# Cross-attention and FFN layer: keys of the first two batches on POOL's queue, one root in the token norm, VectorE in source order, full last key chunks

## The chip, the cores and the metric

The kernel runs on one core of a Trainium2 chip. The metric is device time in microseconds (us) of one execution, as the median of three runs. The profile is one further execution on the same chip. Engines: PE (TensorE), DVE (VectorE), ACT (ScalarE), POOL (GpSimd) and SP (SyncE, which here only issues DMAs); PEld is PE's weight load.

## What is computed

Input x is 8 batches of 100 tokens of width 512 (800 tokens); the context is 8 batches of 722 rows of width 512, with a mask of padded rows. The layers, cut to what matters:

```python
x = x + align(ctx, layernorm(x))       # dynamic programming over 722 by 100 rows, rows of ctx summed along the path
x = x + moe(layernorm(x))              # 16 experts (relu, hidden width 1024), the best 3 of each token by their gates
ln = layernorm(layernorm(x)) * g + b   # a norm of a norm, then gain and bias
xn = layernorm(ctx) * gx + bx
q = rms(ln @ W_q)                      # 8 heads of 64; q and k are normed per head
k, v = rms([xn; ln] @ W_k), [xn; ln] @ W_v
p = softmax(where(mask, q @ k.T, -max))  # 722 context keys, masked, and the batch's own 100 tokens: 822 keys
x = x + (p @ v) @ W_out + b_out        # cross-attention
x = x + ffn(layernorm(x))              # relu, width 2048, 4 experts that differ by a term of rank 4, the best 2
```

All is float32.

## The kernel before

The span falls into stages that follow one another on PE: alignment, with the keys and values of the context computed beside it (to about 600 us); the 16 experts (to 945); the token stage of the cross-attention (979 to 1098); the attention loop (to 1300); the FFN (to the end). A scheduler sets the order of instructions on each engine from the source and its own estimates, except where the source opens a `manual_schedule` for an engine: there that engine follows the source. The attention loop has one for PE, DVE and ACT. Each engine works off its own instructions in order, and waits in order.

**From the experts to the tokens.** Experts' rows go through DRAM: each row block is written to `ys_d` on POOL's queue (L835), and the token stage gathers, for every token, its three rows. Rows over an expert's capacity would be worked off under `tc.If(some > 0)` (L856); in these runs nothing is over, so the branch is passed by, but all engines wait at it. What stands ahead of the If on ACT or SP must be done before any engine goes on.

**`load(b)`** (L907 to L916) begins a batch of the attention: it clears the padding columns of the keys' tile `akt` (L909, POOL), loads 722 keys from `k_d` (L910, SP, 1444 KB), loads the mask words `mw` (L912, SP, the same words to 100 partitions), clears the mask tile `mb` beyond column 722 (L914, POOL) and turns the mask into 0 or minus the largest float (L915, ACT). `akt` has three buffers, `mw` and `mb` two. `early = [load(b) for b in range(2)]` stands ahead of the token loop in the source. The scheduler put these two, and the keys' load of the third batch, ahead of the If.

**The token loop** (L973 to L1066) takes seven tiles of up to 128 tokens. For tile t: three gathers `back` (L978, indirect DMAs on POOL's queue, four buffers), each added into X with its gate on DVE (L982); BN statistics and the norm of the norm, with two roots on ACT (L992, L995) and small DVE steps between them (L993 to L998); `xn` (L1000, DVE); four transposes `pt` (L1003, PE); `xT` (L1005, ACT, four); queries and keys `pqk` (L1013, PE, eight products); squares `asq` (L1015, ACT), their sums `rq` (L1017, DVE), a root (L1018, ACT), a maximum and a reciprocal (DVE), `qn` (L1022, DVE); transposes `apt` (L1030, PE); `qt` and `kl` (L1034, L1036, ACT), `kl` written to `k_d` (L1041, SP). Values `apv` of each batch whose tokens are complete (L1049, PE, one PSUM buffer), `avr` (L1054, DVE), written to `v_d` (L1055, SP). From t = 2 on, two heads' scores `psc` of the first batch (L933, PE) and their row maxima `junk` (L943, DVE). After the loop: `negated` (PE, ACT), `pbo` (L1068, PE), `bo` (L1071, DVE), the seven additions of `bo` into X (L1074, POOL). Then come loads of FFN weights `at_`, `wi` (L1078, L1082, SP), `mt` (L1089, SP) and `mk` from it (L1091, DVE).

**The attention loop** has 32 steps (8 batches by 4 pairs of heads). A step makes the scores `pst` in two groups of key chunks (4 and 3 chunks of 128 keys), adds the negated maxima (`et`, L1123, DVE), takes Exp per chunk (L1129, ACT), sums over chunks (`two`, `ws`, L1153 to L1160, POOL) and multiplies the step before by the values (`apo`, L1141, PE). The chunks start at

```python
STARTS = (0, 128, 256, 384, 512, 640, S2)
```

with S2 = 722, so chunk 5 has 82 keys and chunk 6 the 100 own tokens; `values` loads these two in four pieces (L1103). After two steps `pws` (L1167, PE) spreads the sums.

Of the kernel before, what the change touches and what calls it, by code (L numbers as in the profile page):

```python
# [9 lines left out]
F32 = mybir.dt.float32  # L10
U8 = mybir.dt.uint8
I32 = mybir.dt.int32
AF = mybir.ActivationFunctionType
ALU = mybir.AluOpType
# [3 lines left out]
P = 128  # L18
B, S, D = 8, 100, 512
# [13 lines left out]
KEYS = S2 + S  # L33
MW = (S2 + 3) // 4
KG = ((0, 4), (4, 7))
# [9 lines left out]
KP, KC = 128, 7  # L45
KW = S2 + KP
STARTS = (0, 128, 256, 384, 512, 640, S2)
NCH, CW = 15, 49
# [8 lines left out]
def rows_of(c):  # L57
    return P if c < RC - 1 else RLAST


def key_rows(c):
    return (*STARTS, KEYS)[c + 1] - STARTS[c]


def tok_rows(t):
    return P if t < NT - 1 else NTOK - (NT - 1) * P
# [3 lines left out]
def kernel(  # L70
# [46 lines left out]
    qgs = const.tile([P, 1], F32, name="qgs")  # L117
    nc.vector.tensor_scalar_mul(qgs, gcol[:, 0:1], DH ** -0.5)

    X = state.tile([P, NT, D], F32, name="X")  # L120
# [773 lines left out]
    if True:  # L894
# [8 lines left out]
        if True:  # L903
            ak = attn.enter_context(tc.tile_pool(name="attnk", bufs=2, side="right"))

            def load(b):

                kt = ak.tile([P, NPAIR, KW], F32, tag="akt", name="akt", bufs=3)
                nc.gpsimd.memset(kt[:, :, KEYS:], 0.0)  # L909
                nc.sync.dma_start(out=kt[:, :, :S2], in_=k_d[b, :, :, :S2])  # L910
                mw = ak.tile([S, MW], I32, tag="mw", name="mw")
                nc.sync.dma_start(out=mw, in_=mask[b].partition_broadcast(S))  # L912
                mb = ak.tile([S, KEYS], F32, tag="mb", name="mb")
                nc.gpsimd.memset(mb[:, S2:], 0.0)  # L914
                nc.scalar.activation(mb[:, :S2], mw.bitcast(U8)[:, :S2], AF.Copy, bias=-FMAX, scale=FMAX)  # L915
                return dict(b=b, kt=kt, mb=mb)  # L916
# [5 lines left out]
            def tokens(st):  # L922

                nc.sync.dma_start(out=st["kt"][:, :, S2:KEYS], in_=k_d[st["b"], :, :, S2:])

# [39 lines left out]

            early = [load(b) for b in range(2)]
            with tc.tile_pool(name="qkv", bufs=2, side="right") as qp:
                nc.sync.dma_start(out=wo, in_=w_out.rearrange("(c p) n -> p c n", p=P))
                nc.sync.dma_start(out=bo, in_=b_out.partition_broadcast(P))
                eps = qp.tile([P, 1], F32, name="eps", bufs=1)  # L970
                nc.gpsimd.memset(eps, EPS)
                given = 0
                for t in range(NT):  # L973
                    n = tok_rows(t)
                    cols = ds(t * P, n)
                    for k in range(TOPK):
                        back = qp.tile([P, D], F32, tag="back", name="back", bufs=4)
                        nc.gpsimd.indirect_dma_start(  # L978
                            out=back[:n], out_offset=None, in_=ys_d,
                            in_offset=bass.IndirectOffsetOnAxis(ap=seen[:n, t, k : k + 1], axis=0), bounds_check=NROW,  # L980
                        )
                        nc.vector.scalar_tensor_tensor(  # L982
                            X[:n, t, :], back[:n], gk[:n, t, k : k + 1], X[:n, t, :], ALU.mult, ALU.add
                        )
# [4 lines left out]
                    nc.vector.bn_aggr(mv, st)  # L989
                    rr = qp.tile([P, 4], F32, tag="rr", name="rr")  # L990
                    one, var, two, shift = (rr[:, i : i + 1] for i in range(4))
                    nc.scalar.activation(one, mv[:, 1:2], AF.Sqrt, bias=eps)  # L992
                    nc.vector.reciprocal(one, one)  # L993
                    nc.vector.scalar_tensor_tensor(var, mv[:, 1:2], one, one, ALU.mult, ALU.mult)
                    nc.scalar.activation(two, var, AF.Sqrt, bias=eps)  # L995
                    nc.vector.reciprocal(two, two)
                    nc.vector.tensor_tensor(two, two, one, ALU.mult)
                    nc.vector.scalar_tensor_tensor(shift, mv[:, 0:1], -1.0, two, ALU.mult, ALU.mult)  # L998
                    xn = qp.tile([P, D], F32, tag="xn", name="xn")
                    nc.vector.tensor_scalar(xn, X[:, t, :], two, shift, ALU.mult, ALU.add)  # L1000
                    pt = aps.tile([P, D], F32, tag="tr", name="pt", bufs=1)
                    for dc in range(DC):
# [54 lines left out]
                    if t < 2:  # L1057
                        tokens(early[t])
                    else:
                        st, hp = early[(t - 2) // NPAIR], (t - 2) % NPAIR  # L1060
                        for i, ps in enumerate(scores(st, hp)):
                            largest(st, hp, i, ps)
                for part in range(3):
                    negated(early[0], part)
# [31 lines left out]
            def values(st):  # L1096
                b = st["b"]
                va = at.tile([KP, KC, D], F32, tag="va", name="va")
                nc.sync.dma_start(
                    out=va[:, : KC - 2, :], in_=v_d[b, : STARTS[KC - 2], :].rearrange("(c p) d -> p c d", p=KP)  # L1100
                )
                for c, r0, r1 in ((KC - 2, 0, 80), (KC - 2, 80, key_rows(KC - 2)), (KC - 1, 0, 96), (KC - 1, 96, S)):
                    nc.sync.dma_start(out=va[r0:r1, c, :], in_=v_d[b, STARTS[c] + r0 : STARTS[c] + r1, :])  # L1103
                st["va"] = va
# [14 lines left out]
            def weights(st, hp, c0, c1, ps):  # L1119
# [7 lines left out]
                for c in range(c0, c1):  # L1127
                    n = key_rows(c)
                    nc.scalar.activation(et[:n, c - c0], et[:n, c - c0], AF.Exp, bias=mk[:n, b, c : c + 1])  # L1129
                return et  # L1130

            def products(st, hp, c0, c1, et):
# [4 lines left out]
                for c in range(c0, c1):  # L1137
                    n = key_rows(c)
                    for i in range(2):
                        h = 2 * hp + i  # L1140
                        nc.tensor.matmul(  # L1141
                            st["po"][i * DH : (i + 1) * DH, hp, :], st["va"][:n, c, h * DH : (h + 1) * DH],
                            et[:n, c - c0, i, :], start=c == 0, stop=c == KC - 1,
                        )

            def sums(st, hp, c0, c1, et):
# [8 lines left out]
                two = st["two"]  # L1155
                nc.gpsimd.tensor_tensor(two[:, 0], two[:, 0], et[:, 0], ALU.add)
                nc.gpsimd.tensor_tensor(ws[:, hp], two[:, 0], two[:, 1], ALU.add)
                for c in (1, 2):
                    n = key_rows(KG[1][0] + c)
                    nc.gpsimd.tensor_tensor(ws[:n, hp], ws[:n, hp], et[:n, c], ALU.add)  # L1160

# [274 lines left out]
def _layout(i):  # L1436
# [5 lines left out]
    mask[:, :S2] = np.ascontiguousarray(f["mask_BxS2_bk0"]).view(np.uint8)  # L1442
    keys = np.ones((B, KC + 1, KP), np.uint8)
    keys[:, : KC - 1].reshape(B, -1)[:, :S2] = mask[:, :S2]
    a_t = np.zeros((D, P), np.float32)
# [50 lines left out]
```

## Time and profile before

| | |
|---|---|
| median of 3 runs | 1538.27 us (1536.83 to 1538.72) |
| profiled execution | 1538.33 us |
| its span | 1536.6 us |
| mean granted TensorE clock | 0.949 |
| busy share of the span | PE 90%, DVE 45%, ACT 32%, POOL 28% |
| mean DMA rate | 142 GB/s |

Times of the profile count from the start of the span. A busy PE need not be PE at full clock: the clock that was granted has its own column.

### The profile page before, as it was taken

How to read it: one execution, taken by the hardware profiler on the slowest of the kernel's cores; microseconds unless marked ns; L12 is line 12 of the kernel's file. 1: busy time of each engine (PE TensorE's matmuls, PEld its weight loads, DVE VectorE, ACT ScalarE, POOL GpSimd, SP SyncE). 2: the span in 40 equal slices, each digit the busy share in tenths (PEclk: the TensorE clock that was granted, in tenths of full speed). 3: DMA queues.
4: the chain of work that ended last, by engine and by line, in shares of the span. 5: the costliest groups of instructions: out<-in, count | busy, mean ns of one | idle time of the engine just before them, and what ended most of it. 6: DMA issues, size and time to landing. Idle time of an engine off the chain costs nothing. (4 is left out here: it accounts for less than half of the span.)

```text
span 1536.6 us, 19541 instructions
## 1 busy us (share of the span) xinstructions
PE 1385.6 (90%) x7043; PEld 870.6 (57%) x7043; DVE 684.9 (45%) x1492; ACT 485.2 (32%) x1506; POOL 436.1 (28%) x552
## 2 busy tenths in 40 slices
PE   5979887989799998999999996499999997899998
PEld 4443333444333543899999995144476765544433
DVE  3579999799723251101100100634477773322220
ACT  3424354554522554121122221132354543200000
POOL 1014333545423356000000000600365554322210
PEclk8989899999999998899999998699899999999999
DMA  9861213542655143866567786521544420400000
GB/s 307 298 169 38 78 51 109 167 122 71 207 169 158 56 163 139 291 245 237 204 228 250 260 291 237 143 48 35 194 139 133 134 89 1 164 0 0 1 23 21
DMA packets 120857, 217.78 MB, mean 142 GB/s; under 512 B 47765, under 2 KB 49077, under 8 KB 120629
## 3 DMA queue, kind: packets, MB, share of 16 engines
q1 hardware_dynamic: 103413, 152.54, 30.9%
q0 software_dynamic: 16464, 61.44, 11.5%
q10 hardware_dynamic: 880, 2.51, 0.5%
q8 instruction: 58, 0.95, 0.3%
q14 instruction: 42, 0.34, 0.1%
HBM read 163.92 MB, written 50.86 MB: 140 GB/s over the span
## 5 line engine op out<-in xcount | busy, mean ns | idle before, releaser
L720 PE MATMUL pk<-wc,ctk 128*128 128x512 f32 x384 | 191.9, 641 | 25.8 <-ACT vr L726 22.7
L720 PE MATMUL pv<-wc,ctk 128*128 128x512 f32 x384 | 176.1, 597 | 0.0
L807 PE MATMUL ph<-xe,w1t 128*128 128x192 f32 (+4 forms) x1024 | 171.5, 314 | 1.3 <-DVE xe L798 1.3
L822 PE MATMUL py<-hT,w2t 128*128 128x192 f32 (+4 forms) x1024 | 169.7, 310 | 0.0
L807 PEld LDWEIGHTS ph<-xe,w1t 128*128 128x128 f32 x1024 | 154.4, 192 | 4.7 <-DVE xe L798 1.7
L822 PEld LDWEIGHTS py<-hT,w2t 128*128 128x128 f32 x1024 | 153.1, 191 | 1.8
L720 PEld LDWEIGHTS pk<-wc,ctk 128*128 128x128 f32 x384 | 76.9, 205 | 123.6 <-issue 92.8
L737 ACT ACTIVATE kjunk<-k 128x64 f32<-128x64 f32 x384 | 98.0, 255 | 111.3 <-POOL k L725 95.5
L811 ACT ACTIVATE hT<-ph,b1t 128x192 f32<-128x192 f32 (+4 forms) x128 | 51.8, 404 | 253.4 <-PE ph L807 253.4
L720 PEld LDWEIGHTS pv<-wc,ctk 128*128 128x128 f32 x384 | 73.1, 191 | 91.6 <-issue 88.6
L1129 ACT ACTIVATE et<-et,mk 128x200 f32<-128x200 f32 (+2 forms) x224 | 85.8, 451 | 67.2 <-DVE et L1123 67.1
L725 POOL TENSOR_TENSOR k<-k,kbias 128x512 f32<-128x512 f32 x48 | 71.9, 1503 | 99.1 <-ACT k L724 98.9
L798 DVE COPY xe<-px 128x768 f32<-128x768 f32 (+4 forms) x16 | 14.0, 875 | 185.8 <-PE ph L807 170.4
L835 POOL DMA_DIRECT2D ys_d<-yr x28 | 15.3, 547 | 285.8 <-ACT yr L834 285.8
L1356 PE MATMUL fpb<-xT,wi 128*128 128x400 f32 x256 | 91.5, 507 | 1.0 <-DVE z L1378 1.0
L1405 PE MATMUL fpo<-wot,hw 128*128 128x512 f32 x192 | 84.8, 595 | 0.0
L750 POOL TENSOR_TENSOR k<-k,rk 128x512 f32<-128x512 f32 x48 | 63.7, 1353 | 60.2 <-DVE rk L747 60.2
L440 DVE SCALAR_TENSOR_TENSOR junk<-two_i,path,C 8x735 f32<-8x735 f32 x64 | 74.1, 1157 | 9.7 <-DMA C<-step_d 7.7
L1113 PE MATMUL pst<-qt,akt 64*128 64x100 f32 x896 | 66.3, 282 | 6.8 <-DVE et L1123 6.7
L737 ACT ACTIVATION_READ_ACCUMULATOR kjunk<-k 128x1 f32 x384 | 72.0, 188 | 0.0
L1356 PEld LDWEIGHTS fpb<-xT,wi 128*128 128x128 f32 x256 | 47.0, 190 | 42.5 <-issue 9.4
L943 DVE CUSTOM_DVE_ANT_0 junk<-psc,mb 100x822 f32<-100x822 f32 x64 | 64.2, 1003 | 13.6 <-PE psc L933 13.3
(334 smaller groups left out, 2031.3 us busy)
## 6 DMA issues: line engine op xcount, KB each, us to landing
w1t<-in_w SPq DMA_DIRECT2D x16, 2048.0 KB
w2t<-in_w SPq DMA_DIRECT2D x16, 2048.0 KB
ct<-in_context_t SPq DMA_DIRECT2D x8, 1444.0 KB
ctk<-in_context_t POOLq DMA_DIRECT2D x8, 1444.0 KB
akt<-k_d SPq DMA_DIRECT2D x8, 1444.0 KB
cr<-in_context SPq DMA_DIRECT2D x8, 1280.0 KB
va<-v_d SPq DMA_DIRECT2D x8, 1280.0 KB
v_d<-vr POOLq DMA_DIRECT2D x8, 768.0 KB
```

The costliest lines, as they stand in the source:

```text
L440: nc.vector.scalar_tensor_tensor(junk, two_i1, path[:, j + 1 : j + 2], scol, ALU.is_le, ALU.mult, accum_out=path[:, j : j + 1])
L720: nc.tensor.matmul(ps, ct[:, dc, c * P : (c + 1) * P], wc[:, dc, lo : lo + D], start=dc == 0, stop=dc == DC - 1)
L725: nc.gpsimd.tensor_tensor(kc, kc, kbias, ALU.add)
L737: nc.scalar.activation(junk, k[:, c, h * DH : (h + 1) * DH], AF.Square, accum_out=rk[:, c, h : h + 1])
L750: nc.gpsimd.tensor_tensor(kh, kh, rk[:, c, :].unsqueeze(2).to_broadcast([P, NH, DH]), ALU.mult)
L807: nc.tensor.matmul(ph[:, :cap], st["w1t"][:, dc, hc * P : (hc + 1) * P], st["xe"][:, dc, :cap], start=dc == 0, stop=dc == DC - 1,)
L822: nc.tensor.matmul(py[:, dc, :cap], st["w2t"][:, hc, (2 * dh + dc) * P : (2 * dh + dc + 1) * P], st["hT"][:, hc, :cap], start=hc == 0, sto ...
L943: nc.vector.tensor_tensor_reduce(out=junk, in0=ps.rearrange("p b c -> p (b c)")[:S, :KEYS], in1=st["mb"], scale=1.0, scalar=-FMAX, op0=ALU ...
L1113: nc.tensor.matmul(ps[:, i, (c - c0) * S : (c - c0 + 1) * S], st["kt"][rows, hp, STARTS[c] : STARTS[c] + KP], qt[rows, hp, b * S : (b + 1) ...
L1129: nc.scalar.activation(et[:n, c - c0], et[:n, c - c0], AF.Exp, bias=mk[:n, b, c : c + 1])
L1356: nc.tensor.matmul(pb[:, :N2], wi[fc * P // FQ][:, dc, fc * P % FQ : fc * P % FQ + P], xT[:, dc, hh * N2 : (hh + 1) * N2], start=dc == 0, ...
L1405: nc.tensor.matmul(po[:n], hw[:, fc, t * P : t * P + n], wot[:, fc, :], start=fc == 0, stop=fc == FC - 1)
```

## The change

- `load` takes a queue. The first two batches are now loaded inside the token loop: the keys go out on POOL's queue (`nc.gpsimd`), each issued after the last gather of the next tile (`tc.issue_after`); the mask words stay on SP.
- The keys' tile is 822 wide, without padding columns; the mask word array holds the 100 own tokens too, and so `mb` is written by one activation of 822 columns. The memsets of both are gone.
- The norm of the norm takes one root: variance v gives 1/sqrt((1 + e) v + e e), with e = 1e-5, in place of a root, a reciprocal, a product and a second root and reciprocal. The memset of `eps` moves to the kernel's start.
- In the token loop DVE follows the source. The source takes the gathers, additions and norm of tile t + 1 (`gathered`) ahead of tile t's other work.
- The last two chunks are full: they start at 594 and 694 and overlap their neighbours; the key mask hides the repeated keys. Values load in three pieces instead of five, Exp and products take 128 rows throughout, and the sums of the second group take three POOL operations instead of four.

In the changed program SP's and POOL's orders follow from this: ahead of the If SP issues only the four mask loads; the third batch's keys are SP's first issue after it. POOL issues gathers 1 to 6, keys of batch 0, gathers 7 to 9, keys of batch 1, gathers 10 to 21. PE's, ACT's and DVE's orders in the token stage change too: on PE, `pt` of tile t + 1 and `apt` of tile t follow `pqk` of tile t after one `psc`, and `apv` comes later; on ACT, `xT` of t + 1 stands ahead of the root of `rq` of t; on DVE, `mk` stands ahead of `bo`.

```diff
--- before.py
+++ after.py
@@ -31,7 +31,7 @@
 NH, DH = 8, 64
 NPAIR = NH // 2
 KEYS = S2 + S
-MW = (S2 + 3) // 4
+MW = (S2 + S + 3) // 4
 KG = ((0, 4), (4, 7))
 FE, FF, FTOPK, FR = 4, 2048, 2, 4
 FC = FF // P
@@ -43,8 +43,8 @@
 RC = 6
 RLAST = S2 - (RC - 1) * P
 KP, KC = 128, 7
-KW = S2 + KP
-STARTS = (0, 128, 256, 384, 512, 640, S2)
+
+STARTS = (0, 128, 256, 384, 512, S2 - KP, KEYS - KP)
 NCH, CW = 15, 49
 LANES = NCH + 1
 LAG = NCH - 1
@@ -56,10 +56,6 @@
 
 def rows_of(c):
     return P if c < RC - 1 else RLAST
-
-
-def key_rows(c):
-    return (*STARTS, KEYS)[c + 1] - STARTS[c]
 
 
 def tok_rows(t):
@@ -116,6 +112,9 @@
     nc.sync.dma_start(out=gcol, in_=gamma_cols)
     qgs = const.tile([P, 1], F32, name="qgs")
     nc.vector.tensor_scalar_mul(qgs, gcol[:, 0:1], DH ** -0.5)
+
+    eps = const.tile([P, 1], F32, name="eps")
+    nc.gpsimd.memset(eps, EPS * EPS)
 
     X = state.tile([P, NT, D], F32, name="X")
     nc.gpsimd.memset(X[:, NT - 1, :], 0.0)
@@ -903,16 +902,14 @@
         if True:
             ak = attn.enter_context(tc.tile_pool(name="attnk", bufs=2, side="right"))
 
-            def load(b):
-
-                kt = ak.tile([P, NPAIR, KW], F32, tag="akt", name="akt", bufs=3)
-                nc.gpsimd.memset(kt[:, :, KEYS:], 0.0)
-                nc.sync.dma_start(out=kt[:, :, :S2], in_=k_d[b, :, :, :S2])
+            def load(b, queue=nc.sync):
+
+                kt = ak.tile([P, NPAIR, KEYS], F32, tag="akt", name="akt", bufs=3)
+                queue.dma_start(out=kt[:, :, :S2], in_=k_d[b, :, :, :S2])
                 mw = ak.tile([S, MW], I32, tag="mw", name="mw")
                 nc.sync.dma_start(out=mw, in_=mask[b].partition_broadcast(S))
                 mb = ak.tile([S, KEYS], F32, tag="mb", name="mb")
-                nc.gpsimd.memset(mb[:, S2:], 0.0)
-                nc.scalar.activation(mb[:, :S2], mw.bitcast(U8)[:, :S2], AF.Copy, bias=-FMAX, scale=FMAX)
+                nc.scalar.activation(mb, mw.bitcast(U8)[:, :KEYS], AF.Copy, bias=-FMAX, scale=FMAX)
                 return dict(b=b, kt=kt, mb=mb)
 
 
@@ -921,7 +918,7 @@
             nc.vector.tensor_copy(sel[DH:], ident[DH:, DH : DH + NH].unsqueeze(2).to_broadcast([DH, NH, KP]))
             def tokens(st):
 
-                nc.sync.dma_start(out=st["kt"][:, :, S2:KEYS], in_=k_d[st["b"], :, :, S2:])
+                nc.sync.dma_start(out=st["kt"][:, :, S2:], in_=k_d[st["b"], :, :, S2:])
 
             def scores(st, hp):
 
@@ -963,19 +960,17 @@
                     )
                 nc.scalar.copy(st["nb"][:, :, i, :], pm[:, : NPAIR * S].rearrange("p (c n) -> p c n", c=NPAIR))
 
-            early = [load(b) for b in range(2)]
+            early = []
             with tc.tile_pool(name="qkv", bufs=2, side="right") as qp:
                 nc.sync.dma_start(out=wo, in_=w_out.rearrange("(c p) n -> p c n", p=P))
                 nc.sync.dma_start(out=bo, in_=b_out.partition_broadcast(P))
-                eps = qp.tile([P, 1], F32, name="eps", bufs=1)
-                nc.gpsimd.memset(eps, EPS)
                 given = 0
-                for t in range(NT):
+                def gathered(t):
+
                     n = tok_rows(t)
-                    cols = ds(t * P, n)
                     for k in range(TOPK):
                         back = qp.tile([P, D], F32, tag="back", name="back", bufs=4)
-                        nc.gpsimd.indirect_dma_start(
+                        got = nc.gpsimd.indirect_dma_start(
                             out=back[:n], out_offset=None, in_=ys_d,
                             in_offset=bass.IndirectOffsetOnAxis(ap=seen[:n, t, k : k + 1], axis=0), bounds_check=NROW,
                         )
@@ -987,17 +982,27 @@
                     mv = qp.tile([P, 2], F32, tag="mv", name="mv")
                     nc.vector.bn_stats(st, X[:, t, :])
                     nc.vector.bn_aggr(mv, st)
-                    rr = qp.tile([P, 4], F32, tag="rr", name="rr")
-                    one, var, two, shift = (rr[:, i : i + 1] for i in range(4))
-                    nc.scalar.activation(one, mv[:, 1:2], AF.Sqrt, bias=eps)
-                    nc.vector.reciprocal(one, one)
-                    nc.vector.scalar_tensor_tensor(var, mv[:, 1:2], one, one, ALU.mult, ALU.mult)
-                    nc.scalar.activation(two, var, AF.Sqrt, bias=eps)
+                    rr = qp.tile([P, 2], F32, tag="rr", name="rr")
+                    two, shift = rr[:, 0:1], rr[:, 1:2]
+                    nc.scalar.activation(two, mv[:, 1:2], AF.Sqrt, scale=1.0 + EPS, bias=eps)
                     nc.vector.reciprocal(two, two)
-                    nc.vector.tensor_tensor(two, two, one, ALU.mult)
                     nc.vector.scalar_tensor_tensor(shift, mv[:, 0:1], -1.0, two, ALU.mult, ALU.mult)
                     xn = qp.tile([P, D], F32, tag="xn", name="xn")
                     nc.vector.tensor_scalar(xn, X[:, t, :], two, shift, ALU.mult, ALU.add)
+                    return xn, got
+
+                hand = tc.manual_schedule(engines={mybir.EngineType.DVE})
+                hand.__enter__()
+                xns = {0: gathered(0)}
+                for t in range(NT):
+                    n = tok_rows(t)
+                    cols = ds(t * P, n)
+                    if t + 1 < NT:
+                        xns[t + 1] = gathered(t + 1)
+                    if t < 2:
+                        with tc.issue_after(xns[t + 1][1].ins):
+                            early.append(load(t, nc.gpsimd))
+                    xn = xns.pop(t)[0]
                     pt = aps.tile([P, D], F32, tag="tr", name="pt", bufs=1)
                     for dc in range(DC):
                         nc.tensor.transpose(pt[:, dc * P : (dc + 1) * P], xn[:, dc * P : (dc + 1) * P], ident)
@@ -1060,6 +1065,7 @@
                         st, hp = early[(t - 2) // NPAIR], (t - 2) % NPAIR
                         for i, ps in enumerate(scores(st, hp)):
                             largest(st, hp, i, ps)
+                hand.__exit__(None, None, None)
                 for part in range(3):
                     negated(early[0], part)
 
@@ -1097,10 +1103,10 @@
                 b = st["b"]
                 va = at.tile([KP, KC, D], F32, tag="va", name="va")
                 nc.sync.dma_start(
-                    out=va[:, : KC - 2, :], in_=v_d[b, : STARTS[KC - 2], :].rearrange("(c p) d -> p c d", p=KP)
-                )
-                for c, r0, r1 in ((KC - 2, 0, 80), (KC - 2, 80, key_rows(KC - 2)), (KC - 1, 0, 96), (KC - 1, 96, S)):
-                    nc.sync.dma_start(out=va[r0:r1, c, :], in_=v_d[b, STARTS[c] + r0 : STARTS[c] + r1, :])
+                    out=va[:, : KC - 2, :], in_=v_d[b, : (KC - 2) * KP, :].rearrange("(c p) d -> p c d", p=KP)
+                )
+                for c in (KC - 2, KC - 1):
+                    nc.sync.dma_start(out=va[:, c, :], in_=v_d[b, STARTS[c] : STARTS[c] + KP, :])
                 st["va"] = va
 
             def raw_scores(st, hp, c0, c1):
@@ -1125,8 +1131,7 @@
                     st["nb"][:, hp].unsqueeze(2).to_broadcast([KP, 2, nk, S]), ALU.add,
                 )
                 for c in range(c0, c1):
-                    n = key_rows(c)
-                    nc.scalar.activation(et[:n, c - c0], et[:n, c - c0], AF.Exp, bias=mk[:n, b, c : c + 1])
+                    nc.scalar.activation(et[:, c - c0], et[:, c - c0], AF.Exp, bias=mk[:, b, c : c + 1])
                 return et
 
             def products(st, hp, c0, c1, et):
@@ -1135,12 +1140,11 @@
                     po = aps.tile([P, D], F32, tag="po", name="apo", bufs=1)
                     st["po"] = po[:, : NPAIR * S].rearrange("p (c n) -> p c n", c=NPAIR)
                 for c in range(c0, c1):
-                    n = key_rows(c)
                     for i in range(2):
                         h = 2 * hp + i
                         nc.tensor.matmul(
-                            st["po"][i * DH : (i + 1) * DH, hp, :], st["va"][:n, c, h * DH : (h + 1) * DH],
-                            et[:n, c - c0, i, :], start=c == 0, stop=c == KC - 1,
+                            st["po"][i * DH : (i + 1) * DH, hp, :], st["va"][:, c, h * DH : (h + 1) * DH],
+                            et[:, c - c0, i, :], start=c == 0, stop=c == KC - 1,
                         )
 
             def sums(st, hp, c0, c1, et):
@@ -1153,11 +1157,9 @@
                     nc.gpsimd.tensor_tensor(st["two"], et[:, 0:2], et[:, 2:4], ALU.add)
                     return
                 two = st["two"]
-                nc.gpsimd.tensor_tensor(two[:, 0], two[:, 0], et[:, 0], ALU.add)
+                nc.gpsimd.tensor_tensor(two, two, et[:, 0:2], ALU.add)
                 nc.gpsimd.tensor_tensor(ws[:, hp], two[:, 0], two[:, 1], ALU.add)
-                for c in (1, 2):
-                    n = key_rows(KG[1][0] + c)
-                    nc.gpsimd.tensor_tensor(ws[:n, hp], ws[:n, hp], et[:n, c], ALU.add)
+                nc.gpsimd.tensor_tensor(ws[:, hp], ws[:, hp], et[:, 2], ALU.add)
 
             def spread(st, j):
 
@@ -1440,8 +1442,12 @@
     cols = lambda v: v.reshape(-1, P).T
     mask = np.zeros((B, 4 * MW), np.uint8)
     mask[:, :S2] = np.ascontiguousarray(f["mask_BxS2_bk0"]).view(np.uint8)
-    keys = np.ones((B, KC + 1, KP), np.uint8)
-    keys[:, : KC - 1].reshape(B, -1)[:, :S2] = mask[:, :S2]
+    mask[:, S2:KEYS] = 1
+    keys = np.zeros((B, KC + 1, KP), np.uint8)
+    for c, s in enumerate(STARTS):
+
+        new = max(STARTS[c - 1] + KP if 0 < c < KC - 1 else S2 if c else 0, s) - s
+        keys[:, c, new:] = mask[:, s + new : s + KP]
     a_t = np.zeros((D, P), np.float32)
     b_t = np.zeros((P, FF), np.float32)
     for e in range(FE):
```

## The prediction

> **What bounds the kernel now.** I read the page's slices first. PE is 90% busy over the span, so only stretches in which PE idles can be won. The row of the granted clock falls to 6 in one slice alone (961 to 999 us): the way from the experts' last product into the cross-attention. So I asked for the waits of 940 to 980 us (engine, line, releaser: total, times, longest):
>
> ```profile
> PE pt L1003 <- DVE xn L1000: 33.5, 1, 33.5
> ...
> POOL eps L971 <- DMA akt<-k_d: 13.7, 1, 13.7
> ...
> ACT mb L915 <- DMA mw<-in_mask: 11.7, 2, 8.1
> ```
>
> PE stands still for 33.5 us, POOL for 13.7 of them. The timeline tells the chain (start, duration, engine):
>
> ```profile
> 946.01 0.54 SPq L910 DMA_DIRECT2D akt<-k_d  x1
> 946.55 0.54 POOL L835 DMA_DIRECT2D ys_d<-yr  x1 [1.15 <-ACT yr L834]
> 946.59 1.04 SPq L912 DMA_DIRECT2D mw<-in_mask  x1
> ...
> 958.80 0.81 ACT L915 ACTIVATE mb<-mw 100x722 f32<-100x722 uint8 x1 [3.63 <-DMA mw<-in_mask]
> 960.74 0.10 POOL L971 MEMSET eps<- 128x1 f32 x1 [13.65 <-DMA akt<-k_d]
> 961.56 1.14 POOL L978 DMA_INDIRECT back<-ys_d,seen  x1 [0.72 <-issue]
> ...
> 969.07 0.69 DVE L988 BATCH_NORM_STATS2 st<-X 128x6 f32<-128x512 f32 x1
> ...
> 979.08 1.09 PE L1003 MATMUL pt<-ident,xn 128*128 128x128 f32 x4 [33.49 <-DVE xn L1000]
> ```
>
> The small mask loads mw share the DMA engines with two 1444 KB loads of keys and land 8.7 and 12.2 us after issue. mb2 ends at 959.61, ACT and SP pass the If, all engines go on at 960.2, the first gather is issued at 961.56. The first tile's norm takes 9.3 us from BN_STATS to xn (978.35), since VectorE works off other tiles' additions between its small steps. So the waits named for POOL as "akt" are those behind the If.
>
> **The start.** After, mw loads stand alone on SP. Nearest quiet prices: the last mw load, 3.50 us from issue to landing; the ys_d write of 934.15, 3.05 us. Then mw2, issued by 945.6, lands by 949.1 at most and I take 948.6; mb1 and mb2 follow each other (0.81 us for 722 columns, so 0.92 by estimate for 822), done at 949.7; ys_d, issued 946.55, lands 949.6. In before POOL's first instruction came 1.13 us after mb2's end, and the memset with the 0.72 us behind it is gone. First gather: 950.9 (950.4 to 952.5, the upper end if the third keys, which SP now issues just after the If, slow it). From first gather to BN_STATS lie 7.5 us in the row; then 0.69 + 0.18 + 0.29 (the one root) + 0.15 + 0.15 + 0.52 with handoffs of 0.05 makes 2.4, because the source order leaves no additions in between. PE starts 10.0 after the gather: 960.9 instead of 979.04, **-18.1 us** (-16 to -18.6). The second root, its reciprocal, product and variance (0.29, 0.15, 0.21, 0.15) are inside that.
>
> The keys on POOL's queue: gathers 7 to 9 stand behind the first, 10 to 12 behind the second. Price: 0.79 us of POOL for the issue (row of ctk, L763, same size), 4.2 us of data at the 343 GB/s of 950 to 960 us. Tile 2's xn is wanted some 27 us after PE's start and its gathers land at about 7, so nothing (if that cover were gone, up to 5 us each). The scores that need these keys come 40 us in.
>
> **The token stage.** Until the last scores before pn (1086.41) PE needs 107.4 us in before. Of these it waits 4.7: 4.2 for xT before pqk, 0.5 before apv. With norms early I leave 1.5 of that: -3.2. But the order of the changed program's instructions changes what covers the chain of a tile. Before, around tile 3:
>
> ```profile
> 1033.12 3.60 PE L1013 MATMUL pqk<-wkv,xT 128*128 128x512 f32 x8
> ...
> 1036.82 1.02 ACT L1015 ACTIVATE asq<-pqk 128x1024 f32<-128x1024 f32 x1 [5.14 <-PE pqk L1013]
> ...
> 1039.13 0.22 ACT L1018 ACTIVATE rq<-rq 128x16 f32<-128x16 f32 x1 [1.29 <-DVE rq L1017]
> ...
> 1039.95 1.23 DVE L1022 TENSOR_TENSOR qn<-pqk,rq 128x1024 f32<-128x1024 f32 x1
> ...
> 1042.13 1.04 PE L1030 MATMUL apt<-ident,qn 128*128 128x128 f32 x8
> 1042.34 1.50 ACT L1005 ACTIVATE xT<-pt,lncol 128x128 f32<-128x128 f32 x4 [2.99 <-PE pt L1003]
> ```
>
> From pqk's end (1036.72) to qn's end (1041.18) are 4.5 us: the squares, VectorE's sum (1.22, at 1037.88), the root, two small steps, qn. An apv (3.4), a psc and pt stand between on PE and hide them. In the changed program tiles 2 to 5 run pqk(t), one psc (1.55), pt(t+1) (0.66), apt(t), and only then the other psc and apv. That is 2.2 us of cover. And on ACT the four xT of t+1 (1.50) now stand ahead of the root of rq: pt ends at +2.2, xT at +3.8, where the root could have run at +2.4. The chain becomes 5.9 us, and behind the waiting apt PE's whole queue stands: 5.9 - 2.2 = 3.7 us, four times, +14.8. One apv waits for VectorE to free its PSUM buffer: +0.9. Net **+12.5 us** (bounds: 2.2 us a stall if xT weren't in the way, so +6.5, to +15).
>
> **The clock.** A stall of 3.7 us is long enough to be felt twice. The windows view (PE busy is the second number, PEclk the third from the end):
>
> ```profile
> 1100.25:1103.66 3.41, 1.90 (x26) 1.32 (x24) 3.32 (x6) 2.35 (x4) 3.41 (x4) 1.00 1.02 375
> 1103.66:1107.07 3.41, 3.41 (x19) 1.99 (x18) 1.29 (x3) 2.89 (x9) 3.41 (x4) 0.50 1.07 301
> ```
>
> The granted clock changes on a grid of 3.41 us, and a thin stretch is answered by half clock in the next. I took PE's busy share in every such stretch at full clock: of 14 under one half, 13 were followed by half clock; of 384 over it, 5. A gap of 3.7 us laid anywhere on this grid takes at least 1.85 us from one stretch, so leaves it under half. One stretch at half clock loses 1.7 us of PE's work: 4 x 1.7 = **+6.8 us** (0 to 13.6, where the clock needs a second stretch to come back, as after 260.6).
>
> The Trainium skill ("TensorE: Matmul & The Clock Gate", Part 1) has half rate come after an idle window of some 3.4 us on a free-running grid. Read as a wholly idle window, a 3.7 us gap would cover one in (3.7 - 3.4)/3.4, about one time in ten, and by it this term would be some 0.7 us and the forecast about 1536. The trace speaks against that reading (the stretch above was busy for 1.90 of 3.41 us), and I go by the trace.
>
> **Entry to the attention.** VectorE's order sets mk ahead of bo. From the timeline:
>
> ```profile
> 1098.25 0.69 DVE L1071 TENSOR_TENSOR bo<-bo,pbo 128x512 f32<-128x512 f32 x1 [7.30 <-PE pbo L1068]
> 1099.29 1.04 DVE L1091 TENSOR_SCALAR mk<-mt 128x64 f32<-128x64 uint8 x1 [0.35 <-DMA mt<-in_mask_t]
> ...
> 1114.93 0.56 PE L1167 MATMUL pws<-ws,ones 128*64 128x200 f32 x4 [2.51 <-POOL ws L1160]
> ```
>
> bo then starts about 2.0 later (after mk's end at 1100.3), POOL's seven additions of bo (8.61 us) too, and PE already waits 2.51 us for the first ws behind them. Each step's sums take one operation fewer (two of 1.03 and two of 0.61 instead of one and four: 0.2 less), which gives back 0.1 to 0.4: **+1.9 us**. The wait of 4.4 us can bring one more thin stretch: **+0.9** (half of 1.7).
>
> **Edits at nothing.** 16 memsets of about 0.2 on POOL, which idles 72%; the eps memset, now at kernel start; the mask 100 columns wider (0.1 of ACT per batch, a batch ahead); two value loads fewer per batch on SP; full last chunks: Exp takes 452 ns on 128 rows and 446 on fewer, the products 254 and 249. If these covers were gone: 32 steps x 2 Exp x 6 ns, under 1 us. In the loop the later fold of the sums can delay ws by 0.15 a step, off PE's path but in steps 2 of a batch; the shorter sums speak the other way: 0 (-2 to +1).
>
> **Sum**: -18.1 + 12.5 + 6.8 + 1.9 + 0.9 = +4.0. The profiled execution took 1538.33 us (span 1536.6 and 1.7 around it), 0.06 over the median: 1542.3.
>
> **Rivals.**
> 1. The clock holds through the stalls (six of seven stretches 50 to 60% busy stayed at full clock): -18.1 + 12.5 + 1.9 = -3.7, 1534.6. Not slower. It decides where the stalls are under some 2 us, or split so that no stretch falls below half. Against it: 13 of 14. Chance 0.20.
> 2. No stalls, PE's queue is covered as before: -18.1 - 3.2 + 1.9 = -19.4, 1519 (to 1528 with half of the stalls). Against it: the order of PE's and ACT's instructions is fixed. 0.08.
> 3. Each dip lasts two stretches: 6.8 more, 1549. 0.14.
> 4. The first gather isn't earlier, since something else holds the If: only the shorter norm, -7.5, remains, and the sum is +14.6, 1553. For it: ys_d's landing and SP's own waits also stand ahead of the gather; against: the quiet prices. 0.06.
>
> **How the numbers follow.** My forecast (1538.5 to 1546) has 0.52. The range reaches from 1532 to 1549: rival 1 within, 2 and 4 left out. About 0.2% (3.1 us) is what a measurement of this kernel can tell from no change. Faster by more: rival 2, over half of rival 1 and a tail, 0.22; within: the rest of 1 and a third of the forecast, 0.24; slower: 0.54.
>
> **What would show it.** Right: first gather near 951, PE's pt near 961, four waits of apt for qn of 3 to 4 us, half clock after each, pn within 3 us of 1086, bo after mk. Wrong: first gather after 953; waits of apt under 2 us; a clock of 1.00 all through 990 to 1080; a loop (first to last pws) that changes by over 2 us.

## The result and the profile after

The changed kernel takes 1557.08 us (1556.26 to 1561.35, 4 runs) against 1537.97 us before: a ratio of 1.0129, 95% interval 1.0112 to 1.0146, so some 20 us slower. I had forecast slower by 4 us, with 1549 as the upper end of the range; the sign was right, the size and the range were not.

The profiled execution took 1561.35 us, its span is 1559.6 us, 23.0 over before's. I set both spans off at the same marks: the last `pyr` of the experts, the first gather, the token stage's first product (`pt`), `pn` (the end of the stage's scores), the first `pws`, the end.

| us between marks | before | after | difference |
|---|---|---|---|
| start to last pyr | 945.3 | 948.4 | +3.1 |
| to first gather | 16.3 | 6.9 | -9.3 |
| to first pt | 17.5 | 11.9 | -5.7 |
| to pn (token stage) | 107.3 | 139.0 | **+31.6** |
| to first pws | 28.5 | 30.6 | +2.1 |
| to the end | 421.7 | 422.9 | +1.2 |

The first row lies ahead of the change: in the runs below this mark falls anywhere between 942.0 and 947.8, so I take its 3.1 us for the spread of executions (this one was the slowest of its four, and its 948.4 lies just above them). The rest is +19.9; the medians differ by 19.1.

The start went as read. Of the waits (940 to 1000 us):

```profile
PE pt L1008 <- DVE xn L991: 18.5, 1, 18.5
...
POOL back L973 <- DMA mw<-in_mask: 5.1, 1, 5.1
...
ACT mb L912 <- DMA mw<-in_mask: 1.2, 1, 1.2
```

PE's 33.5 us have become 18.5 and ACT's waits for mask words have shrunk from 11.7 to 1.2: they land 2.6 to 3.0 us after issue. The token stage is where the time went. Its waits of PE (980 to 1110 us), and PE's timeline around the first of them:

```profile
PE apt L1035 <- DVE qn L1027: 14.5, 4, 3.6
PE apv L1054 <- DVE avr L1059: 0.9, 1, 0.9
```

```profile
1007.68 0.66 PE L1008 MATMUL pt<-ident,xn 128*128 128x128 f32 x4
1011.96 1.94 PE L1035 MATMUL apt<-ident,qn 128*128 128x128 f32 x8 [3.62 <-DVE qn L1027]
1013.83 3.06 PE L930 MATMUL psc<-akt,qt 64*100 64x512 f32 x4
1016.82 5.93 PE L1054 MATMUL apv<-wkv,xT 128*100 128x512 f32 x8
```

Four waits of apt, 3.62 us each: these are the stalls of the prediction. But behind each, apt takes 1.94 us and not 1.04, psc 3.06 and not 1.6, and much of apv nearly its double. The windows view (length, PE busy, PEld, DVE, ACT, POOL, PEclk, DMA share, GB/s) shows how long the clock stays down:

```profile
1007.74:1011.15 3.41, 0.60 (x5) 0.36 (x4) 1.83 (x4) 1.61 (x5) 0.00 (x0) 1.00 0.00 0
1011.15:1014.56 3.41, 2.60 (x9) 1.98 (x10) 2.19 (x4) 0.63 (x2) 0.00 (x0) 0.50 0.20 60
1014.56:1017.98 3.42, 3.42 (x6) 1.18 (x5) 1.06 (x3) 0.64 (x2) 0.00 (x0) 0.50 0.34 77
1017.98:1021.39 3.41, 3.41 (x6) 1.16 (x5) 3.01 (x5) 0.23 (x1) 2.21 (x2) 0.50 0.41 27
1021.39:1024.80 3.41, 3.41 (x10) 1.45 (x9) 0.87 (x3) 0.07 (x1) 1.17 (x2) 1.00 0.67 209
```

One thin stretch (0.60 us busy), then three at half clock, the second and third of them wholly busy. All four waits are followed by 10.24 us at half clock (from 1011.15, 1035.04, 1062.35 and 1086.24). Over the whole stage PE's idle and busy time part cleanly (before, then after):

```profile
979.00:1086.40 107.40, 102.58 (x288) 44.19 (x288) 46.83 (x104) 29.24 (x64) 10.61 (x10) 0.98 0.22 56
```

```profile
967.00:1106.20 139.20, 122.56 (x289) 51.78 (x289) 53.29 (x96) 28.51 (x60) 18.13 (x16) 0.83 0.26 74
```

The same work: idle 16.6 instead of 4.8 us (+11.8), busy 122.6 instead of 102.6 (+20.0). The second number is the clock: in the first dip PE is busy for 2.60 + 3.42 + 3.41 = 9.43 us, and at full clock this work takes half, so 4.7 us are lost; four such dips make 18.9 of the 20.0.

### The profile page after: what moved, and what is told of

Read it like the earlier page. It is cut to its first block, busy times and chain, and to the rows that moved or that the text cites. A ratio compares the mean times of both kernels' runs of the same rounds, so it can differ in the third digit from the quotient of the medians.

```text
span 1559.6 us, 19417 instructions
## 1 busy us (share of the span) xinstructions
PE 1409.7 (90%) x7043; PEld 881.1 (56%) x7043; DVE 684.0 (44%) x1471; ACT 485.4 (31%) x1499; POOL 429.7 (28%) x506
## 4 chain that ended last, share of the span: by engine, by line
PE 47%; issue 21%; DVE 16%; DMA 10%; POOL 3%; ACT 3%; SPq 1%; DVEq 0%; POOLq 0%; ACTq 0%
PE fpb L1358 6%; PE fpo L1407 5%; PE psc L930 4%; PE ph L806 3%; PE pqk L1018 3%; PE py L821 3%; DVE C L394 3%; PE pst L1119 3%; DMA cr<-in_context 3%; PE apv L1054 2%; DMA ct<-in_context_t 2%; PE pe L482 2%; PE apo L1145 2%; PE py L1188 2%; PE pk L719 2%
## 5 line engine op out<-in xcount | busy, mean ns | idle before, releaser
L1134 ACT ACTIVATE et<-et,mk 128x200 f32<-128x200 f32 x224 | 86.2, 453 | 67.4 <-DVE et L1129 67.4
L834 POOL DMA_DIRECT2D ys_d<-yr x28 | 15.3, 547 | 296.8 <-ACT yr L833 296.8
L1119 PEld LDWEIGHTS pst<-qt,akt 64*128 64x128 f32 x896 | 57.4, 192 | 24.8 <-DVE et L1129 15.7
```

What stands on the lines that cost most here:

```text
L1119: nc.tensor.matmul(ps[:, i, (c - c0) * S : (c - c0 + 1) * S], st["kt"][rows, hp, STARTS[c] : STARTS[c] + KP], qt[rows, hp, b * S : (b + 1) ...
L1134: nc.scalar.activation(et[:, c - c0], et[:, c - c0], AF.Exp, bias=mk[:, b, c : c + 1])
```

## Experiments

Theory A: the order of the token stage makes the loss, by PE's waits and the half clock behind them; the start is a gain. Rival B: another part (keys on POOL's queue, full chunks) makes it. All runs are against the kernel before on the same chip (its median between 1537.3 and 1538.3).

**e1: the change without VectorE's order**

```diff
-                hand = tc.manual_schedule(engines={mybir.EngineType.DVE})
-                hand.__enter__()
...
-                hand.__exit__(None, None, None)
```

> The changed kernel, with DVE left to the scheduler in the token stage again; all else stays. Theory A (the order of the token stage makes the loss: four waits of apt of 3.6 us and the half clock behind each): the scheduler puts apv or a second psc between pqk and apt again, the waits vanish, the clock stays full from 1000 to 1085 us, the early start stays, and the time is about 1557 - 14 - 17 = 1526 (1521 to 1532). Rival B (the keys on POOL's queue or the full chunks make the loss): the time stays within 5 us of 1557.

Measured 1524.38 us, ratio 0.9918 (0.9893 to 0.9943): 14 us faster than before. PE's waits from 960 to 1115 us begin so:

```profile
PE pt L1006 <- DVE mv L984: 21.5, 1, 21.5
PE pst L1116 <- DVE et L1126: 5.1, 2, 4.2
PE pws L1166 <- POOL ws L1159: 2.9, 1, 2.9
```

No wait of apt is left; the stage takes 104.5 us and its clock is whole from 972.2 to 1084.8. The first pt comes 15.3 us after the first gather, not 11.9: that is what VectorE's order had been good for.

**e2: VectorE's order alone, on the kernel before**

```diff
-                for t in range(NT):
+                def gathered(t):
...
+                hand = tc.manual_schedule(engines={mybir.EngineType.DVE})
+                hand.__enter__()
+                xns = {0: gathered(0)}
+                for t in range(NT):
...
+                    if t + 1 < NT:
+                        xns[t + 1] = gathered(t + 1)
```

> The kernel before, with one part of the change alone: the token loop takes the gathers and norm of tile t+1 first, and DVE follows that source; keys on SP ahead of the If, two roots, short last chunks. Theory A: PE's order has apt behind one psc and pt in tiles 3, 4 and 5, so two or three waits of 2.3 to 3.7 us and as many dips of the clock, some 7 us each, against some 8 us from the shorter first norm and early xn: 1545 to 1552. Rival B: no loss from the order, the norm's gain alone, 1530 to 1533.

Measured 1558.24 us, ratio 1.0137 (1.0103 to 1.0171): worse than the upper end of what I gave. PE's waits from 975 to 1105 us begin with

```profile
PE apt L1040 <- DVE qn L1032: 10.9, 3, 3.6
```

Three waits of 3.6 us, each followed by 10.24 us at half clock; the stage takes 130.3 us (+22.9), against a first pt 6.5 us sooner after the first gather. One part of the change costs what the whole change costs; e1 and e2 together settle A against B.

**e7 and e8: the load move alone, the full chunks alone, on the kernel before**

```diff
-                nc.sync.dma_start(out=kt[:, :, :S2], in_=k_d[b, :, :, :S2])
+                queue.dma_start(out=kt[:, :, :S2], in_=k_d[b, :, :, :S2])
...
-            early = [load(b) for b in range(2)]
+            early = []
...
+                    if 0 < t < 3:
+                        with tc.issue_after(got.ins):
+                            early.append(load(t - 1, nc.gpsimd))
...
```

> The kernel before with the load move alone: the first two batches' keys on POOL's queue behind the gathers of tiles 1 and 2, mask words on SP; memsets, two roots, short chunks and free VectorE as before. Theory A: the If opens 9 us earlier (first gather 6.9 us after the last pyr, not 16.3), the order of tiles is the scheduler's: 1538 - 9 + 0 to 2 = 1529 to 1531. Rival B (keys on POOL's queue cost as much as they save): 1535 to 1540.

```diff
-STARTS = (0, 128, 256, 384, 512, 640, S2)
+STARTS = (0, 128, 256, 384, 512, S2 - KP, KEYS - KP)
...
```

> The kernel before with the full last chunks alone (three value loads instead of five, Exp and products on 128 rows, three sums instead of four). My prediction had 0 (-2 to +1) for it: 1536 to 1539. Rival (the later start of the sums lengthens the loop, in which the changed kernel took 1.4 us more): 1539.5 to 1542.

The load move: 1525.2 us, ratio 0.9912 (0.9895 to 0.9928), more than I gave it. The first gather comes 6.5 us after the last pyr instead of 16.3, and the stage shrinks by 5.2 to 102.1 us; 3.7 of that is idle time of PE (1.1 us in the stage, before 4.8). I read this as gathers that begin earlier than PE's work and keep ahead of it. The chunks: 1536.31 us, ratio 0.9991 (0.9979 to 1.0002), no difference, as forecast. With e2 the parts give -12 - 1 + 20 = +7 (the one root, e11 below, changes nothing clear of noise), where the change is +19. They do not simply add. By the stage's own length the gap lies there: -5.2 (e7) and +22.9 (e2) against +31.6. The change has a fourth wait of apt, in tile 2, which with its dip costs some 3.6 + 5 us, and most of the 5 us by which e7 shortens the stage is idle time that e2's order takes away as well. This is a reckoning; no run tests it.

**e11: one root alone, on the kernel before**

```diff
-                nc.gpsimd.memset(eps, EPS)
+                nc.gpsimd.memset(eps, EPS * EPS)
...
-                    nc.scalar.activation(one, mv[:, 1:2], AF.Sqrt, bias=eps)
-                    nc.vector.reciprocal(one, one)
-                    nc.vector.scalar_tensor_tensor(var, mv[:, 1:2], one, one, ALU.mult, ALU.mult)
-                    nc.scalar.activation(two, var, AF.Sqrt, bias=eps)
...
+                    nc.scalar.activation(two, mv[:, 1:2], AF.Sqrt, scale=1.0 + EPS, bias=eps)
...
-                    nc.vector.tensor_tensor(two, two, one, ALU.mult)
```

> The kernel before with the one root alone. Small steps of 0.29 + 0.15 + 0.21 + 0.15 us go, and with them up to 4 us of waiting between them in the first norm: PE's start 1 to 4 us after an unchanged first gather, 1534 to 1537. Rival (VectorE's additions fill the place): 1537.5 to 1539.

1539.27 us, ratio 1.0013 (0.9996 to 1.0031): no difference, as the rival has it (0.3 us above the range I gave it). The first pt comes 13.3 us after the gather, 4.2 sooner; the stage then takes 111.3 us, 3.9 more. PE only waits later, still for xT and, new, at an apv (955 to 1090 us):

```profile
PE pqk L1009 <- ACT xT L1001: 3.8, 3, 1.6
PE apv L1045 <- DVE avr L1050: 2.4, 1, 2.4
```

**e3, e5, e6: what follows a wait.** Here PE and ACT are in a hand order too, tile by tile as in the changed kernel (e3); e5 and e6 move one thing each (the remarks behind # are mine).

```diff
-                hand = tc.manual_schedule(engines={mybir.EngineType.DVE})
+                hand = tc.manual_schedule(engines={mybir.EngineType.PE, mybir.EngineType.DVE, mybir.EngineType.Activation})
...
+                    products_of(t)        # pqk, asq, sum
+                    head_scores(t, 0)     # psc of one head
+                    if t + 1 < NT:
+                        turned(t + 1)     # pt, xT
+                    normed(t)             # root of rq, maximum, reciprocal, qn
+                    heads_of(t)           # apt, qt, kl
+                    head_scores(t, 1)
+                    own_values(t, B)      # apv, avr
...
```

> The changed kernel with PE and ACT of the token stage written out by hand too, in the order the changed kernel has in tiles 2 to 5 (pqk, one psc, pt of the next tile, apt, the other psc, apv; xT ahead of the root of rq). It is the base for the runs that move one thing in this order. Theory A: the same four waits of 3.6 us and the same dips of 10.2 us; 1550 to 1557 (the mask's activation falls behind the If, which can bring up to 3 us). Rival B says nothing else.

```diff
                     heads_of(t)
-                    head_scores(t, 1)
                     own_values(t, B)
+                    head_scores(t, 1)
```

> As e3, but behind the waiting apt stands apv (128 rows by 100 columns of weights, 3.4 us) and then the other psc (64 rows by 100 columns); in e3 psc stood first in tiles 2 to 5. The waits of apt stay at 3.6 us. Theory A1 (the clock comes back only after a stretch full of products on all 128 rows; psc holds it down): in tiles 2 to 5 the half clock lasts 3.4 or 6.8 us, not 10.2, and the token stage shortens by 4 x 1.7 to 3.4, from 152 to 138 to 146 us. Rival A2 (the length of the dip is set by the wait alone): it stays at 10.2 us in tiles 2 to 5, the stage at 150 to 154.

```diff
                     products_of(t)
+                    normed(t)
                     head_scores(t, 0)
...
-                    normed(t)
                     heads_of(t)
```

> As e3, but on ACT the root of rq stands ahead of xT of the next tile. Theory A: the wait of apt in tiles 2 to 5 falls from 3.6 to 2.3 us (the chain 4.5 less 2.2 of cover), six waits give back some 8 us, and as a wait with its transposes covers less of a stretch, one or two dips vanish: a stage of 130 to 145 us. Rival (xT is not on the chain): waits of 3.6 us, stage 150 to 154.

e3 took 1573.25 us, ratio 1.0221 (1.0188 to 1.0255), 16 us more than the changed kernel: tiles 0 and 1 have no apv ahead of apt any more, so there are six waits (22.6 us), and in tiles 2 to 5 another 1.8 us each where pqk waits for a PSUM buffer that the second head's maximum holds. As a copy of the changed kernel it failed; as a base it serves, because its own waits differ in what follows them. In tiles 0 and 1 apv follows apt, and half clock lasts 3.41 us; in tiles 2 to 5 psc follows, and it lasts 10.24 us each time. For tile 2, the stretch that holds the wait and the next two:

```profile
1013.97:1017.38 3.41, 0.98 (x6) 0.42 (x4) 1.82 (x4) 1.61 (x5) 0.00 (x0) 1.00 0.00 0
1017.38:1020.79 3.41, 2.23 (x9) 1.93 (x10) 1.04 (x1) 0.25 (x1) 0.00 (x0) 0.50 0.00 0
1020.79:1024.21 3.42, 3.42 (x5) 1.03 (x5) 0.00 (x0) 1.02 (x2) 0.00 (x0) 0.50 0.30 67
```

In e5, with apv behind apt in all tiles, the same place of tile 4:

```profile
1057.97:1061.38 3.41, 0.43 (x4) 0.19 (x2) 1.83 (x4) 1.61 (x5) 0.00 (x0) 1.00 0.00 0
1061.38:1064.79 3.41, 2.77 (x10) 2.24 (x11) 0.49 (x1) 0.80 (x2) 0.00 (x0) 0.50 0.00 0
1064.79:1068.20 3.41, 3.41 (x9) 1.16 (x8) 0.29 (x1) 0.47 (x1) 0.00 (x0) 1.00 0.33 77
```

The wait is as long (3.62 us) and the first stretch as thin, yet the clock is back after one stretch. Of e5's dips in tiles 2 to 5 three last 3.41 us and one 6.83; its stage takes 136.1 us instead of 152.2, one execution 1553.4 us. That is below the range I gave A1, since 6.2 of the 16.1 us are idle time: the waits of 1.8 us at pqk shrink to 0.3 as well. A1 holds in its main point: what follows the wait sets how long the clock stays down.

apv and psc both have 100 columns of weights and up to 512 moving; they differ in rows, 128 against 64. That the rows are the reason is the nearest reading; no run changed them alone, but the traces speak for it in two more places. The transposes apt stand first in both kinds of dip, and busy time alone does not decide: above, 2.77 us of apt and apv were enough for full clock, while in the changed kernel 3.07 us of apt and psc were not:

```profile
1035.04:1038.45 3.41, 3.07 (x10) 2.21 (x11) 0.79 (x2) 1.10 (x2) 0.00 (x0) 0.50 0.20 60
1038.45:1041.86 3.41, 3.41 (x5) 1.04 (x5) 0.00 (x0) 0.17 (x1) 0.00 (x0) 0.50 0.42 77
```

And in the attention loop the psc of two heads, 64 rows each, run two at a time: at half clock eight products take 2.88 us, where four of one head took 3.06. In the profile of before a stretch full of such pairs was followed by full clock:

```profile
1104.40 2.88 PE L933 MATMUL psc<-akt,qt 64*100 64x512 f32 x8
...
1103.66:1107.07 3.41, 3.41 (x19) 1.99 (x18) 1.29 (x3) 2.89 (x9) 3.41 (x4) 0.50 1.07 301
1107.07:1110.48 3.41, 3.41 (x60) 3.02 (x58) 2.66 (x6) 1.30 (x4) 3.25 (x5) 1.00 0.92 284
```

e6 gave waits of 2.45 us in tiles 2 to 5 instead of 3.62, as computed (2.3), but a stage of 148.4 us, outside what I had for it, and 1574.54 us in one execution. All six waits are still followed by half clock, of 6.8 or 10.2 us in tiles 2 to 5: the shorter wait saved itself and no dip. Two of the four in tiles 2 to 5 came behind stretches in which PE was busy for more than half, which the rule of the prediction does not cover; 1.14 and 1.62 us of them were psc on 64 rows:

```profile
1037.97:1041.38 3.41, 1.73 (x8) 0.75 (x6) 2.25 (x4) 2.12 (x6) 0.00 (x0) 1.00 0.00 0
...
1089.17:1092.58 3.41, 2.37 (x9) 0.99 (x8) 1.65 (x3) 1.80 (x4) 0.00 (x0) 1.00 0.00 0
```

**e4: the waits covered by order**

```diff
                     products_of(t)
+                    normed(t)
+                    own_values(t, 1)
                     head_scores(t, 0)
                     if t + 1 < NT:
                         turned(t + 1)
-                    normed(t)
                     heads_of(t)
                     head_scores(t, 1)
                     own_values(t, B)
```

> As the run before, but PE's order per tile is pqk, apv, one psc, pt of the next tile, apt, the other psc, and ACT takes the root of rq ahead of xT. Theory A: 5.6 us of PE work lie between pqk's end and apt, more than the chain's 4.5, so no wait of apt over 0.5 us, no stretch at half clock between 1000 and 1085, and the stage takes some 104 us: about 1557 - 14.5 - 17 - 3 = 1522 (1517 to 1527). Rival B: the waits go but the time falls by no more than the 14.5 us that they sum to, 1542 or more, since the clock's dips have another cause.

1527.18 us, ratio 0.9929 (0.9904 to 0.9953), as A has it, at the upper end of its range: the same parts as e3, another order on PE and ACT, 46 us less. Two waits of apt of 0.6 and 0.7 us are left, in the first tiles, a little more than I had allowed; the stage takes 106.8 us.

**e9 and e10: VectorE's order where it is of use**

```diff
-                hand = tc.manual_schedule(engines={mybir.EngineType.DVE})
-                hand.__enter__()
-                xns = {0: gathered(0)}
+                with tc.manual_schedule(engines={mybir.EngineType.DVE}):
+                    xns = {0: gathered(0), 1: gathered(1)}
...
-                hand.__exit__(None, None, None)
```

> The changed kernel, with DVE by the source for the first two tiles' gathers and norms only, and free from there. Theory A (the source order helps where nothing covers VectorE, the first norm, and costs where it lets PE wait): PE starts 12 us after the first gather as in the changed kernel, not 15.3 as in e1; no wait of apt; 1524 - 3.4 = 1520 to 1522. Rival (any hand order in this stage brings the waits back): 1530 or more.

```diff
...
+                    if t == 2:
+                        with tc.issue_after(xns[t + 1][1].ins):
+                            third = keys(2, nc.gpsimd)
...
```

> As e9, and the third batch's keys also on POOL's queue, behind the gathers of tile 3. Theory A: the first gathers no longer share the DMA engines with 1444 KB, land 3.5 us after issue as in e4, not 6.4, and PE starts 10 us after the first gather: another 2 us, 1518 to 1520. Rival (the transfer is hidden anyway): within 1 us of e9.

e9 beats both kernels: 1515.93 us, ratio 0.9856 (0.9824 to 0.9889), 22 us under before and 41 under the change, and some 4 us under the range I gave it. The first pt comes 12.4 us after the first gather and 18.9 after the last pyr; then the stage is one unbroken run:

```profile
963.07:1066.52 103.45, 102.35 (x289) 44.46 (x289) 51.07 (x97) 28.56 (x60) 17.74 (x16) 0.97 0.36 102
```

In e9 `bo` also came ahead of `mk` again, and pn to pws takes 27.6 us. e10 does not add to it: 1517.51 us, ratio 0.9859 (0.9828 to 0.9891), 1.6 us above e9: theory A is out, and the rival's 1 us not quite met. The gathers land in 3.5 us as computed and pt starts 2.3 us sooner after its gather, but PE then waits for the tiles behind:

```profile
PE pt L1013 <- DVE xn L994: 16.4, 1, 16.4
PE pqk L1023 <- ACT xT L1015: 5.8, 3, 3.1
```

In e9 that second line is 1.1 us. The sooner start is given back, as in e11. I read this as a stage bound by the arrival of the next tiles' rows; no run tests it.

## Why the prediction was wrong, point by point

- **The clock: the term that failed.** I had +6.8 us, four dips of one stretch of 3.41 us, with 13.6 as the bound for a second stretch. The dips lasted three stretches each and cost +20.0 us of PE's time. The step behind it was that a stretch in which PE works brings the clock back. The first half of the rule, a stretch under half busy is followed by half clock, held again (after: 21 of 22 such stretches at full clock), though in e6 two stretches above half were followed by it too, and the row that I showed for the rule (1100.25, 1.90 of 3.41 us) is itself 56% busy, the one of rival 1's seven that fell. The second half I had not counted out: I read off when the clock goes, and of its return only that it can take a second stretch. In the profile of before the return after 1090.01 took two stretches, the first wholly busy, with `pnb` and `apt` in it; that row was there. e3 against e5 shows that the kind of work decides: behind the wait stood a psc on 64 rows.

```profile
1090.01:1093.42 3.41, 3.41 (x17) 2.65 (x17) 0.94 (x2) 1.12 (x3) 0.00 (x0) 0.50 1.06 410
1093.42:1096.83 3.41, 3.41 (x6) 1.34 (x5) 0.00 (x0) 0.00 (x0) 0.00 (x0) 0.50 0.69 232
```

- **The Trainium skill on this point** ("TensorE: Matmul & The Clock Gate", Part 1) has the clock come back after one busy window. The stretch 1014.56 to 1017.98 was wholly busy and the clock stayed at 0.50 in the next; the measurement decides. Its Part 4 says that transposes do not count as busy in the same way. Here the measurement speaks against it: in the profile of before one stretch at half clock held transposes alone (`pt`, L164), and the clock was whole in the next:

```profile
1315.29:1318.70 3.41, 3.27 (x15) 2.91 (x16) 1.61 (x4) 2.08 (x5) 0.00 (x0) 0.50 0.96 215
1318.70:1322.11 3.41, 3.41 (x16) 2.20 (x15) 0.00 (x0) 0.85 (x2) 0.00 (x0) 1.00 1.02 414
```

- **The stalls: right.** Four waits of 3.62 us against 3.7, one of 0.9 at an apv, idle +11.8 us against +12.5. The chain of asq, sum, xT, root and qn against psc and pt of cover was read off the kernel before, and e6 shows its xT term: 3.62 falls to 2.45.
- **The start: right in kind, 3 us too high.** -15.0 against -18.1. The first gather came 6.9 us after the last pyr (I had 5.6: ys_d took 4.61 us to land, not 3.05). PE's start came 11.9 after the gather, not 10.0, since the third keys on SP held the first gathers for 6.36 us; e10, without them, has 10.1. I had named this only in the range.
- **Entry to the attention: right.** As the timeline shows, `bo` began behind `mk`, 1.8 us after pbo's end (1118.75), and PE waited 3.54 us for the first ws; +2.1 against +2.8. `mk` stands ahead of `bo` in e1 and e7 too, where VectorE is free, so it is not the hand order that puts it there:

```profile
1120.45 0.20 DVE L1097 TENSOR_SCALAR mk<-mt 128x64 f32<-128x64 uint8 x1 [6.12 <-DMA mt<-in_mask_t]
1120.56 0.68 DVE L1077 TENSOR_TENSOR bo<-bo,pbo 128x512 f32<-128x512 f32 x1
...
1136.73 0.56 PE L1169 MATMUL pws<-ws,ones 128*64 128x200 f32 x4 [3.54 <-POOL ws L1162]
```

- **Chunks: right**, nothing (e8). The memsets and the wider mask no run tests by themselves.
- **The rivals.** Rival 3 (each dip lasts two stretches, 1549, chance 0.14) was the nearest, and still a stretch short. Rival 1, the clock holds, is out: every wait of apt of 2.4 us or more, in five kernels, was followed by half clock. Rival 2's time of 1519 lies between those of e1 (1524) and e9 (1516), in which the waits of apt are gone because the order was changed; the rival had them gone without that.

## What to carry to other kernels

An engine put into source order moves the others too: read, for the engine that bounds the stage, which of its instructions stand between the start of a dependent chain and the wait for its end, and compare their sum with the chain. On PE, price a wait by what comes after it as well: here 3.6 us of waiting cost another 5 us of half clock. Use a hand order where nothing else covers the latency (the first norm: e9) and leave the rest to the scheduler where it had covered it.

## What the runs showed of the hardware that I had not expected

- After a thin stretch the granted clock came back after 3.41 us (once 6.83) when products on 128 rows followed the wait and its transposes, and after 10.24 us when products on 64 rows did, though PE was busy throughout the second of these stretches (e5, e3).
- A stretch of transposes alone, 3.27 of 3.41 us busy at half clock, was followed by full clock (before, 1315.29).
- A wait of 2.45 us between transposes was followed by half clock each of four times (e6).
- 1444 KB of keys in flight bring a 256 KB gather from 3.5 us to 6.4 us from issue to landing (e10, after), and two such loads the mask words from 2.6 to 3.0 us (after) to 8.7 and 12.2 us (before).
